# Layer 3's scans: two additions over states moved to GpSimd, one copy of exponents moved to VectorE

## The chip, the cores and the metric

The kernel runs on one core of a Trainium2 chip. A core has a matrix engine (TensorE, in the profile PE; its weight loads are PEld), three engines for elementwise work (VectorE = DVE, ScalarE = ACT, GpSimd = POOL) and SyncE (SP), which here only issues transfers. Each engine takes its instructions in the order of the program; engines wait for one another on semaphores. TensorE multiplies into PSUM, a small memory [...] that VectorE and ScalarE can read; everything else lies in SBUF (on chip) or DRAM. The metric is the time of one execution in microseconds (us), the median of three runs.

## The reference

The network has four layers on an input of 4 x 96 x 56 x 56 in float32. Layer 0 is attention, layer 1 a selective scan in eight directions, layer 2 a local attention. Layer 3, in which the change lies, contains a scan in four directions (rows, rows backwards, columns, columns backwards) over L = 56 x 56 = 3136 positions for 192 channels d and 16 states n, written with cumulative sums:

```
dlt = softplus(dt_proj(...) + dt_proj_b)
dA  = dlt[..., None] * A_log[None, :, :, None, :]
phi = jnp.exp(-jnp.cumsum(dA, axis=3))
dbx = dlt[..., None] * b[...] * xs[..., None]
h   = phi * jnp.cumsum(dbx / (phi + 1e-12), axis=3)
y   = jnp.einsum('bkdln,bknl->bkdl', h, c) + Ds
```

The sum over the 16 states n in the last line is the part that line 1446 to 1450 of the kernel compute; the exponents cumsum(dA) are what line 1375 copies.

## The kernel before

`network` (line 1662) runs the layers one after the other; `layer3` (line 1516) calls `cumulative` (line 1168), the stage that the change touches. It handles two directions at a time (k = 0, 1, then 2, 3). Positions are cut into chunks of 93 (`TW`), a chunk into three blocks of 31 positions (`TB`) plus one row of carry. A block holds 4 batch entries x 32 rows on the 128 partitions and 6 x 16 x 32 = 3072 values along the free axis. There are 2 x 34 = 68 chunk pairs, and so 68 x 3 x 2 = 408 blocks, the two directions in turn.

What happens to one block, with the names used below:

- `zhalf(st, h)`, line 1358, for h = 0 and 1: 48 matrix products of 32 x 32 x 256 (line 1367) give half of the block's exponents (8 of the 16 states) in the PSUM tile `z`, which has three banks and one buffer. Line 1375 copies the half, 128 x 1536 values, from PSUM to the block's `phi` in SBUF. "z0" and "z1" are the products of the two halves, "copy 0" and "copy 1" their copies. z1 can't start before copy 0 has emptied `z`.
- `inverse`, line 1383: ScalarE's sigmoid of `phi` into `w`. `phis`, line 1391: ScalarE's exponential of `phi` in place. The two need different tables (ACT_TABLE_LOAD).
- `weights`, lines 1399 to 1408: 16 small products into PSUM (`misc`), and on GpSimd a memset and two multiplications for `m`.
- `into_sum`, line 1415: VectorE multiplies `w` (SBUF) by `misc` (PSUM), 128 x 3072. Behind it SP's queue issues a transfer (line 1416) that puts the carry from DRAM (`l3cr`) into rows 31, 63, 95, 127 of `w`.
- `sums(st, q)`, line 1427, q = 0 to 3: 64 products give the cumulative sums of four states in PSUM (`q`, two buffers). They need `w` with its carry.
- `times(st, q)`, line 1436: VectorE multiplies them by `phi`, 128 x 768, result in `phi`.
- `carry`, line 1440: SP issues the transfer of the block's last row to `l3cr`.
- `out`, line 1442: three additions halve the 16 states to 2 (lines 1446, 1447 and 1448, into the tile `t`), a fourth (line 1450) makes `y`; SP issues four stores of `y` (line 1458).

The order on every engine is the order in which the program is written (`in_order`, line 53, ties each instruction to the one before it on its engine). The loop at line 1481 runs over pairs of blocks (`now`), with the next pair (`nxt`) and the one after (`third`) in work. One iteration handles block S of `now`, C = the block after S, and T = a block of `third`. VectorE's order in one iteration is: `times` S 0 and 1, `into_sum` C, `times` S 2 and 3, (scans of the next chunk), `out` S. TensorE's: `misc` of C, `sums` S 2 and 3, z0 of T, (products of the next chunk), z1 of T, `sums` C 0 and 1. ScalarE's: `inverse` or `phis` of one block, copy 0 of T, `inverse` or `phis` of the second block, copy 1 of T. GpSimd's: `m` of C, (work of the next chunk), `out` S. SP's: the carry into `w` of C (line 1416), the carry of S (line 1440), (loads of the next chunk), the stores of `y` (line 1458).

The next chunk is prepared in twelve steps (`tick`, lines 1503 and 1511), two an iteration, so that the six iterations of a chunk differ. In order of time: loads of `u`; two iterations with products of line 1229; one with the products of line 1256 and three softplus (line 1261 to 1263), the iteration in which `tick` says "wide" since these products use `z`'s banks, and z1 of T is put behind `sums` C; then two with a scan over time for one direction each: GpSimd's `du` (line 1298), VectorE's addition (line 1303, two inputs in SBUF), its scan (line 1311, two inputs in SBUF) and a small copy (line 1313), placed behind z1 and ahead of `out`. I call the six: loads, products 1, products 2, wide, scan 1, scan 2.

Of the kernel before, what the change touches and what calls it, by code (L numbers as in the profile page):

```python
# [11 lines left out]
ALU = mybir.AluOpType  # L12
# [19 lines left out]
def view(ap, offset, dims):  # L32

    return bass.AP(ap.tensor, ap.offset + offset, [ap.ap[0], *dims])
# [35 lines left out]
class Net:  # L70
# [1097 lines left out]
    def cumulative(self, us, dram):  # L1168


        nc, tc = self.nc, self.tc
# [6 lines left out]
        with in_order(tc), ExitStack() as cx:  # L1178
# [179 lines left out]
            def zhalf(st, h):  # L1358
                s, i = st["s"], st["i"]
                lo = TW - TB * (i + 1) if s["rev"] else TB * i  # L1360
                st["lo"] = lo
                z = psz.tile([128, 3, 2, 8, 32], F32, name="z")
                for dh in range(2):
                    for b in range(B):
                        for p in range(3):
                            ps_ = slice(32 * p, 32 * p + 32)
                            nc.tensor.matmul(  # L1367
                                z[32 * b : 32 * b + 32, p, dh].rearrange("p n d -> p (n d)"),
                                s["s"][ps_, dh, b, lo : lo + 32],
                                st["ad"][ps_, dh, 8 * h : 8 * h + 8, :].rearrange("p n d -> p (n d)"),  # L1370
                                start=True, stop=True,
                            )
                if h == 0:
                    st["phi"] = big.tile([128, 3, 2, NS, 32], F32, name="phi", bufs=5)
                nc.scalar.copy(  # L1375
                    st["phi"][:, :, :, 8 * h : 8 * h + 8, :].rearrange("p a b n d -> p a b (n d)"),
                    z.rearrange("p a b n d -> p a b (n d)"),
                )
# [63 lines left out]
            def out(st):  # L1442
                s, i, lo, k = st["s"], st["i"], st["lo"], st["k"]
                phi = st["phi"].rearrange("p a b n d -> p (a b) (n d)")
                t = p2.tile([128, 6, 8 * 32], F32, name="t", bufs=1)
                nc.vector.tensor_tensor(t, phi[:, :, 0:256], phi[:, :, 256:512], ALU.add)
                nc.vector.tensor_tensor(t[:, :, 0:128], t[:, :, 0:128], t[:, :, 128:256], ALU.add)  # L1447
                nc.gpsimd.tensor_tensor(t[:, :, 0:64], t[:, :, 0:64], t[:, :, 64:128], ALU.add)  # L1448
                y = p2.tile([128, DI], F32, name="y")
                nc.gpsimd.tensor_tensor(  # L1450
                    view(y, 0, [[32, 3], [96, 2], [1, 32]]),
                    view(t, 0, [[512, 3], [256, 2], [1, 32]]), view(t, 32, [[512, 3], [256, 2], [1, 32]]),
                    ALU.add,
                )
                a, e = max(lo, s["off"]), min(lo + TB, s["off"] + s["tv"])
                at = s["t0"] + a - s["off"]
                for b in range(B):
                    nc.sync.dma_start(
                        ys[k][b, at : at + e - a, :], y[32 * b + a - lo : 32 * b + e - lo, :]
                    )  # L1460
# [9 lines left out]
            for st in (*now, *nxt):  # L1470
                zhalf(st, 0)
                zhalf(st, 1)
# [8 lines left out]
            while now[0] is not None:  # L1481
                third = draw()
                for i, st in enumerate(now):
                    coming_up = (now[1], nxt[0])[i]
                    what = (inverse, phis)[i]
                    if nxt[0] is not None:
                        what(nxt[0])
                    if coming_up is not None:
                        weights(coming_up)
                    times(st, 0)  # L1490
                    times(st, 1)
                    sums(st, 2)
                    sums(st, 3)
                    if third[i] is not None:
                        zhalf(third[i], 0)
                    if nxt[1] is not None:
                        what(nxt[1])
                    if coming_up is not None:
                        into_sum(coming_up)
                    times(st, 2)  # L1500
                    times(st, 3)
                    carry(st)
                    wide = tick()[1]
                    if third[i] is not None and not wide:
                        zhalf(third[i], 1)
                    if coming_up is not None:
                        sums(coming_up, 0)
                        sums(coming_up, 1)
                    if third[i] is not None and wide:
                        zhalf(third[i], 1)  # L1510
                    tick()
                    out(st)
# [288 lines left out]
```

## Time and profile before

| | |
|---|---|
| time, median of 3 runs | 16318.02 us (16299.98 to 16343.79) |
| the profiled execution's own time | 16344.06 us |
| its span, first to last instruction | 16342.0 us |
| mean granted TensorE clock | 0.916 of full |
| the stage of the change, first to last row of line 1415 | 10712.4 to 15499.7 us |
| in the stretch 10700 to 15500 (4800 us) busy: PE, DVE, ACT, POOL | 4172, 4153, 4240, 1788 us |
| mean granted clock in that stretch | 0.93 |
| rows of line 1446 and 1447 (VectorE), mean | 408 x 1755 ns, 408 x 958 ns |
| rows of line 1448 and 1450 (GpSimd), mean | 408 x 998 ns, 408 x 590 ns |
| rows of line 1375 (ScalarE), mean | 816 x 1427 ns |
| rows of line 1436 and 1415 (VectorE), mean | 1632 x 953 ns, 408 x 3346 ns |
| rows of line 1311 (VectorE) and 1298 (GpSimd), median, mean | 136 x 1720 ns, 136 x 1807 ns |

A row of the timeline gives the start, the duration, the engine, the line, the operation, the tiles (out<-in), the shape and, in brackets, how long the engine stood idle before it and whose end released it. Rows of the same line close together are merged (x2). The view by windows gives, for each stretch of time, its length and the busy time of every engine in it, and then the granted clock (PEclk, 1.00 is full).

### The profile page before, as it was taken

The page shows a single profiled execution, that of the slowest core. Times are in us where ns is not written, and L with a number is a line of the kernel's source. Part 1 is how long each engine was busy: PE and PEld are TensorE (multiplying, and loading weights), DVE is VectorE, ACT ScalarE, POOL GpSimd, SP SyncE. Part 2 cuts the span into 40 slices and gives each one's busy share as a digit, 9 for nine tenths or more (in the row PEclk, how much of TensorE's full clock was granted, in tenths as well). Part 3 has the DMA queues.
Part 4 walks back from the last instruction along what each step waited for, and adds up shares of the span by engine and source line. Part 5 has one row for each costly group of instructions (what it writes and reads, how often), then busy time and mean ns, then how long its engine had stood idle before and what let it go on. Part 6 is the DMA issues. An engine that isn't in the chain of part 4 may idle for free.

```text
span 16342.0 us, 501766 instructions
## 1 busy us (share of the span) xinstructions
PE 13255.0 (81%) x222032; PEld 8983.5 (55%) x222032; DVE 13647.4 (84%) x15363; ACT 12214.4 (75%) x15540; POOL 7905.1 (48%) x4079
## 2 busy tenths in 40 slices
PE   8999977777777777777776678878888888888876
PEld 4333326666666666666665555446666656566543
DVE  8666549999999999999998666768888888888866
ACT  0465448999999999999998245478888888888822
POOL 0000028888888888888887022123333333333300
PEclk7999889999999999999999579989999999999977
DMA  0000034333444443434444910222122222222122
GB/s 15 1 1 1 16 137 100 92 92 92 102 105 105 104 93 93 95 92 103 104 106 105 220 41 10 63 61 50 48 51 50 50 50 49 50 50 51 41 67 65
DMA packets 821406, 1152.54 MB, mean 71 GB/s; under 512 B 309360, under 2 KB 728720, under 8 KB 807456
## 3 DMA queue, kind: packets, MB, share of 16 engines
q1 hardware_dynamic: 759872, 1055.38, 26.6%
q10 hardware_dynamic: 53984, 45.77, 1.2%
q8 instruction: 1746, 28.61, 0.8%
q0 software_dynamic: 5376, 19.27, 0.4%
q14 instruction: 428, 3.51, 0.1%
HBM read 842.93 MB, written 277.18 MB: 69 GB/s over the span
## 4 chain that ended last, share of the span: by engine, by line
PE 34%; DVE 29%; ACT 20%; issue 12%; DMA 4%; POOL 1%; SPq 1%; DVEq 0%; ACTq 0%; POOLq 0%
DVE q L634 17%; PE q L1427 7%; ACT ht L659 5%; PE s L233 4%; ACT e L622 3%; PE d L413 3%; ACT phi L1375 3%; DVE w L1415 3%; PE z L1367 2%; PE acc L251 2%; PE m L196 2%; ACT w L1383 2%; PE y L671 2%; PE t L557 2%; PE t L650 2%
## 5 line engine op out<-in xcount | busy, mean ns | idle before, releaser
L614 POOL TENSOR_TENSOR q<-du,bm 128x1792 f32<-128x1792 f32 x1344 | 5348.3, 4026 | 3.1 <-DMA bm<-bc 3.1
L634 DVE TENSOR_TENSOR_SCAN q<-e,state,q 128x448 f32<-128x448 f32 x4608 | 4876.8, 1124 | 145.9 <-ACT e L622 141.9
L622 ACT ACTIVATE e<-dl,na 128x448 f32<-128x448 f32 x5376 | 3354.9, 640 | 173.7 <-DVE q L634 117.8
L671 PE MATMUL y<-ht,cd 128*32 128x64 f32 x75264 | 1838.4, 225 | 1470.2 <-ACT ht L659 1469.6
L650 PE MATMUL t<-ident,q 128*128 128x128 f32 x18816 | 2626.8, 293 | 93.7 <-issue 77.6
L1427 PE MATMUL q<-w,m 32*32 32x192 f32 x52224 | 2573.4, 348 | 125.8 <-DVE phi L1436 72.9
L650 PEld LDWEIGHTS t<-ident,q 128*128 128x128 f32 x18816 | 2391.2, 203 | 325.3 <-issue 203.3
L659 ACT COPY ht<-t 128x896 f32<-128x896 f32 x2688 | 2428.6, 904 | 101.2 <-PE t L650 70.6
L671 PEld LDWEIGHTS y<-ht,cd 128*32 128x32 f32 x75264 | 1400.3, 110 | 1948.2 <-ACT ht L659 1930.7
L1427 PEld LDWEIGHTS q<-w,m 32*32 32x32 f32 x52224 | 1873.5, 113 | 738.1 <-issue 182.2
L1436 DVE TENSOR_TENSOR phi<-q,phi 128x768 f32<-128x768 f32 x1632 | 1513.5, 953 | 523.9 <-PE q L1427 498.3
L1448 POOL TENSOR_TENSOR t<-t 128x384 f32<-128x384 f32 x408 | 407.2, 998 | 2977.2 <-DVE t L1447 2977.2
L241 ACT ACTIVATE e<-s 128x896 f32<-128x896 f32 (+1 forms) x1050 | 921.8, 915 | 913.7 <-PE m L196 516.2
L1367 PE MATMUL z<-ad,sm 32*32 32x256 f32 x39168 | 1277.1, 391 | 396.2 <-ACT phi L1375 382.6
L208 DVE TENSOR_REDUCE pm<-m 128x1 f32<-128x448 f32 (+1 forms) x1700 | 997.8, 618 | 688.6 <-PE m L196 641.4
L1375 ACT COPY phi<-z 128x1536 f32<-128x1536 f32 x816 | 1164.5, 1427 | 528.6 <-PE z L1367 528.4
L1415 DVE TENSOR_TENSOR w<-w,misc 128x3072 f32<-128x3072 f32 x408 | 1365.3, 3346 | 83.9 <-PE misc L1399 46.9
L1383 ACT ACTIVATE w<-phi,lntiny,w_k_rmask 128x3072 f32<-128x3072 f32 x408 | 1203.1, 2949 | 2.6
L196 PE MATMUL m<-ka,qa 32*128 32x448 f32 (+1 forms) x3400 | 1165.9, 628 | 9.0 <-DVE pm L208 7.5
L1391 ACT ACTIVATE phi<-phi,w_k_nmask 128x3072 f32<-128x3072 f32 x408 | 1165.6, 2857 | 2.4
L1367 PEld LDWEIGHTS z<-ad,sm 32*32 32x32 f32 x39168 | 709.1, 104 | 658.9 <-ACT phi L1375 465.2
L292 POOL DMA_DIRECT2D x<-xc x28 | 14.5, 517 | 2153.7 <-DVE xc L291 2152.8
(254 smaller groups left out, 18732.7 us busy)
## 6 DMA issues: line engine op xcount, KB each, us to landing
bm<-bc SPq DMA_DIRECT2D x896, 448.0 KB
cm<-cd SPq DMA_DIRECT2D x544, 186.0 KB
l1y<-out SPq DMA_DIRECT2D x672, 96.0 KB
l1y<-out SPq DMA_DIRECT2D x672, 72.0 KB
y<-l1y ACTq DMA_DIRECT2D x224, 168.0 KB
l3y<-y SPq DMA_DIRECT2D x1616, 23.2 KB
w<-l3cr SPq DMA_DIRECT2D x408, 48.0 KB
l3cr<-phi SPq DMA_DIRECT2D x408, 48.0 KB
```

What stands on the lines that cost most here:

```text
L614: nc.gpsimd.tensor_tensor(q, spread(s["du"][:, j, :], ng), s["bm"][g], ALU.mult)
L622: nc.scalar.activation(e[:, :CH], s["dl"][:, j, :], AF.Exp, scale=na[:, s["k"], j, n : n + 1])
L634: nc.vector.tensor_tensor_scan(a, e, a, first, ALU.mult, ALU.add)
L650: nc.tensor.transpose(flat(t)[:, 128 * c : 128 * c + 128], view(q, h * NC2 + c, [[NC, 128]]), self.ident,)
L659: nc.scalar.copy(t, flat(s["t", j, g, h])[:, : NC2 * 128])
L671: nc.tensor.matmul(s["y", j][r : r + 32, c // 4, 64 * half : 64 * half + 64], s["cd"][:, half, g, c, :], s["t", j, g, h][:, 128 * i + 64 * ...
L1367: nc.tensor.matmul(z[32 * b : 32 * b + 32, p, dh].rearrange("p n d -> p (n d)"), s["s"][ps_, dh, b, lo : lo + 32], st["ad"][ps_, dh, 8 * h ...
L1375: nc.scalar.copy(st["phi"][:, :, :, 8 * h : 8 * h + 8, :].rearrange("p a b n d -> p a b (n d)"), z.rearrange("p a b n d -> p a b (n d)"),)
L1383: nc.scalar.activation(w.rearrange("p a n d -> p (a n d)"), st["phi"].rearrange("p a b n d -> p (a b n d)"), AF.Sigmoid, bias=lntiny, scal ...
L1415: nc.vector.tensor_tensor(st["w"], st["w"], ut, ALU.mult)
L1427: nc.tensor.matmul(qp[bs, n, :DI], st["m"][bs, 4 * q + n, :], st["w"][bs, :, 4 * q + n, :], start=True, stop=True,)
L1436: nc.vector.tensor_tensor(ph, view(st[q], 0, [[256, 4], [32, 6], [1, 32]]), ph, ALU.mult)
```

## The change

Three calls change their engine; no shape, tile, buffer count or place in the program changes.

```diff
@@ zhalf
                 if h == 0:
                     st["phi"] = big.tile([128, 3, 2, NS, 32], F32, name="phi", bufs=5)
-                nc.scalar.copy(
+                (nc.scalar.copy if h == 0 else nc.vector.tensor_copy)(
                     st["phi"][:, :, :, 8 * h : 8 * h + 8, :].rearrange("p a b n d -> p a b (n d)"),
                     z.rearrange("p a b n d -> p a b (n d)"),
                 )
@@ out
                 t = p2.tile([128, 6, 8 * 32], F32, name="t", bufs=1)
-                nc.vector.tensor_tensor(t, phi[:, :, 0:256], phi[:, :, 256:512], ALU.add)
-                nc.vector.tensor_tensor(t[:, :, 0:128], t[:, :, 0:128], t[:, :, 128:256], ALU.add)
+                nc.gpsimd.tensor_tensor(t, phi[:, :, 0:256], phi[:, :, 256:512], ALU.add)
+                nc.gpsimd.tensor_tensor(t[:, :, 0:128], t[:, :, 0:128], t[:, :, 128:256], ALU.add)
                 nc.gpsimd.tensor_tensor(t[:, :, 0:64], t[:, :, 0:64], t[:, :, 64:128], ALU.add)
```

Copy 1 goes from ScalarE to VectorE, where its place is behind `times` S 2 and 3 and ahead of the scan of the next chunk. The first two additions of `out` go from VectorE to GpSimd, where all four now stand in a row. The transfers that depend on them (the stores of `y` on SP's queue) keep their place in that queue.

## The prediction

> **What bounds the kernel now.** I read the page first: no engine is full over the span (PE 81%, DVE 84%, ACT 75%), so the stage has to be read by itself. Its length is 408 blocks; the starts of line 1415's rows give each iteration's length. Averaged over the inner 66 or so chunks, in us: loads 11.31, products 1 10.07, products 2 10.11, wide 15.13, scan 1 12.42, scan 2 11.42; sum 70.5 a chunk. The view by windows of one chunk (scan 1, scan 2, loads, products 1, products 2, wide) shows why they differ:
>
> ```profile
> core 0: us, PE busy (x) PEld busy (x) DVE busy (x) ACT busy (x) POOL busy (x), PEclk, DMA share, GB/s
> 12001.84:12014.90 13.06, 10.71 (x303) 8.76 (x302) 11.50 (x10) 13.00 (x9) 3.05 (x5) 0.87 0.07 20
> 12014.90:12026.31 11.41, 8.78 (x252) 6.25 (x248) 11.31 (x11) 10.04 (x6) 3.99 (x4) 1.00 0.07 19
> 12026.31:12038.29 11.98, 10.02 (x244) 7.17 (x240) 9.63 (x9) 10.52 (x6) 6.20 (x11) 0.86 0.28 68
> 12038.29:12048.47 10.18, 10.16 (x268) 6.88 (x264) 9.54 (x9) 7.78 (x7) 1.74 (x4) 1.00 0.09 24
> 12048.47:12058.59 10.12, 10.12 (x268) 6.86 (x264) 9.62 (x8) 10.09 (x8) 4.10 (x6) 1.00 0.09 25
> 12058.59:12072.59 14.00, 12.29 (x244) 7.64 (x240) 9.71 (x8) 11.14 (x9) 7.31 (x8) 0.88 0.52 123
> ```
>
> Only scan 2 is full on VectorE (11.31 of 11.41). Products 1 and 2 are a chain: `into_sum` C 3.34, carry into `w` by DMA 3.2, `sums` C 0 and 1 2.75, the last `times` 0.9: 10.2. Wide, and often scan 1 and loads, contain half-speed TensorE. So VectorE's time is worth money in two of six iterations at most. Next I read the timeline of scan 2, from `into_sum` C on:
>
> ```profile
> 12014.90 3.34 DVE L1415 TENSOR_TENSOR w<-w,misc 128x3072 f32<-128x3072 f32 x1
> ...
> 12018.16 1.82 DVE L1436 TENSOR_TENSOR phi<-q,phi 128x768 f32<-128x768 f32 x2
> ...
> 12018.37 1.44 ACT L1375 COPY phi<-z 128x1536 f32<-128x1536 f32 x1 [1.34 <-PE z L1367]
> ...
> 12019.86 1.36 PE L1367 MATMUL z<-ad,sm 32*32 32x256 f32 x48 [1.53 <-ACT phi L1375]
> 12019.89 0.16 DVE L1303 TENSOR_TENSOR dl<-dl,tot 96x8 f32<-96x8 f32 x1
> ...
> 12020.09 1.72 DVE L1311 TENSOR_TENSOR_SCAN sm<-starts,dl 96x752 f32<-96x752 f32 x1
> ...
> 12021.93 1.75 DVE L1446 TENSOR_TENSOR t<-phi 128x1536 f32<-128x1536 f32 x1
> ```
>
> To see here: VectorE ends `times` S 3 at 12019.9 (5.0 after the start of `into_sum`), but z1 ends only at 12021.22 (6.3), since it waited for copy 0. Last, the only place where VectorE works on two SBUF inputs while GpSimd works, near the stage's start:
>
> ```profile
> 10751.25 1.73 DVE L1303 TENSOR_TENSOR dl<-dl,tot 96x8 f32<-96x8 f32 x1 [9.14 <-POOL du L1298]
> 10753.01 2.68 DVE L1311 TENSOR_TENSOR_SCAN sm<-starts,dl 96x752 f32<-96x752 f32 x1
> 10755.72 0.83 DVE L1313 COPY tot<-sm 96x8 f32<-96x8 f32 x1
> ```
>
> The same three take 0.16, 1.72 and 0.17 elsewhere. Each ends when a GpSimd instruction (`du`, then line 1407, then line 1408, itself 2.35 in place of 1.05) has ended: they exclude each other, and GpSimd gets in between each two of the three. At 10671 the small copy takes 1.55 behind `du` twice.
>
> **Part 1, the additions.** VectorE loses 1.755 + 0.958 = 2.71 a block. GpSimd's price, from its rows 128x192 0.590, 128x384 0.998, 128x1344 3.055, 128x1792 4.02 (2.15 ns a value): 128x1536 3.47, 128x768 1.82. So `out` takes 3.47 + 1.82 + 1.0 + 0.59 + gaps = 7.2 from the end of `times` S 3, and `y` is ready at 5.05 + 7.2 = 12.3 in place of 9.5. GpSimd's load is 4.5 + 5.3, about 9.9 a block: under every iteration's length, if barely. Behind `y` in SP's queue stand four issues (1.4, to 13.7) and then the next carry into `w`, wanted at 10.1 + 3.4 = 13.5: 0.2 late, once in products, +0.3 a chunk. `phi` is read until 8.6, and its buffer is written next at 13.6: free of cost.
>
> **Part 2, copy 1.** ScalarE loses 1.43 a block (of 10.55). VectorE gains a copy from PSUM: the nearest rows are its copies of line 684 (128x384 0.544) and 260 (128x448 0.617); by the slope between those two (73 ns for 64 values) 128x1536 gives 1.86, by that of line 1446 and 1447 (1.04 ns a value) 1.75. I take 1.75, since rows with PSUM inputs (line 1436, 0.953) and without (line 1447, 0.958) cost the same there; the upper end adds 0.1. So VectorE's own sum falls by only 0.95. But the copy must wait for z1, and it stands ahead of the next scan and of `times` C.
>
> - Products, loads: z1 ends at 6.3 to 6.5, copy to 8.1 to 8.3, `sums` C 0 ends at 8.0, `sums` C 1 at 9.3. `times` C 1 starts at 9.3 as before: nothing gained, nothing lost.
> - Scans, without exclusion: 6.4 + 1.75 + 2.04 (scan) + 1.73 = 11.9 against 11.41: the wait of 1.4 exceeds the 0.95.
> - Wide: z1 ends 0.6 before the next `into_sum` today, as `times` C are long done. Now z1 is followed by copy 1.75 + 0.1 and two `times` 1.8, less the 0.6 and less 0.2 (copy 0 is earlier with a lighter ScalarE): +2.9, to 18.0.
>
> **Part 3, exclusion.** In scan 1 and 2 GpSimd is now in `out` (5.05 to 12.3) when VectorE wants line 1303, 1311 and 1313. The page SBUF — State Buffer of the Trainium skill, section "Who interferes with whom", speaks against the change here: a VectorE instruction with two SBUF inputs and a GpSimd instruction that reads SBUF block each other for a whole instruction, while one with a single SBUF input doesn't collide. The rows above are that, with short GpSimd instructions; so by them: copy 1 ends at 8.2, line 1303 waits for the first addition to 8.6; second addition to 10.5; scan to 12.25; third addition to 13.25; line 1313 to 13.4; `times` to 15.15. Were only the rest of the running addition lost, it would be 12.4; were there none, 11.9. I take 15.15, because in four cases of four in the trace GpSimd slipped in. Copy 1, `into_sum` and `times` have one input in PSUM; line 684's copy, under GpSimd's line 614 all the time, keeps 0.56.
>
> **The clock.** TensorE now idles 2.2 ahead of scan 1 (two `times` and a copy behind z1) and some 4 ahead of scan 2 and loads. The page TensorE: Matmul & The Clock Gate, section "Why this matters for your kernels", says that idle gaps up to about 3 us do no harm. The trace differs: in wide the gap between z0 and line 1256's products is 1.7 to 2.0, and every wide iteration measured has half clock. By the rule scan 1 stays at 15.15; by the row, half of them (as 61% of scan 1 today) lose 0.7, since slow `sums` push z0, z1 and copy 1: 15.5. Scan 2, idle 4, is 15.85 by both; loads go from 11.31 to 12.0 (its value with half clock today).
>
> **Sum.** Per chunk: wide +2.9, scan 1 +3.1, scan 2 +4.4, loads +0.7, products +0.3: +11.4. Times 67 (the last chunk prepares none): +760. Against the profiled execution's own 16344 that is 17104; against the median of 16318, 26 lower, **17078**; I say 17075.
>
> **The rivals.**
> - *No slipping in* (GpSimd doesn't get in between, or `out` is past when the scan comes): scans 12.4 and 12.3, so wide +2.9, scan 1 0, scan 2 +0.9, loads +0.3, products +0.3: +4.4, 16610. For it: only four cases, at the stage's start. Against: each of them.
> - *SP's queue*: if GpSimd's strided additions cost 2 us more than by the straight line (the row 128x384 is at 2.6 ns a value), the carry is 2.2 late in every short iteration and each second one pays: +3 more a chunk, and +2 in each scan: 17550 at most. Against: the rows of strided inputs lie within 0.03 of the line.
> - *Not slower: copy 1 is hidden.* If copy 0 came so early that z1 ended with `times` S 3, VectorE's 0.95 would be won in the scans (10.5), half clock would be gone from loads (10.27) and scan 1, and wide would keep 15.1: 66.6 a chunk, -3.9, 16060. It decides at z1 ending before 5.0 + 0.95 = 5.95, with no exclusion. The trace says 6.3, and z0 alone is 3.4 behind `into_sum`'s start. With the clock alone at full in wide (15.6 with the copy) and no exclusion it would be level with today, 16300.
>
> **How the numbers follow.** Exclusion as worked out, with more or less of the clock: 0.64, 16850 to 17300. No slipping in: 0.2. SP's queue: 0.1. Not slower: 0.06, of which 0.03 faster. The range reaches from within the second case, 16650, to 17350. A measurement can tell some 0.3% (49 us) from no change: slower 0.94, same 0.03, faster 0.03.
>
> **What would show it.** Right: line 1446 on GpSimd at 3.5, 1447 at 1.8; line 1303 and 1311 on VectorE far above 0.16 and 1.72 in most of the 136; scan iterations near 15; wide near 18; copy 1 on VectorE idle 1.3 before it by PE z; products still 10.1. Wrong: line 1303 and 1311 unchanged (then 16610); SP waiting for `y` with line 1416 issued late in products; a clock above 0.93 in the stage.

## The result, and the profile after

The changed kernel takes 17045.03 us (median of 4 runs, 17032.57 to 17049.84) where the kernel before takes 16315.32 (median of 4, 16299.98 to 16343.79): ratio 1.044, 95% interval 1.0427 to 1.0453. The profiled execution took 17032.57 with a span of 17030.8 and a mean granted clock of 0.909. The stage, first to last row of line 1415, went from 4787.3 us to 5537.2 (10647.8 to 16185.0): +749.9 us. The rest of the profiled span was 61 us shorter: the layers ahead of the stage, which the change doesn't touch, ended earlier. In the traces of this case the stage begins anywhere from 10638 to 10712, a spread that no term of the forecast contained.

Iteration lengths, mean over the inner chunks in us; in brackets, how much of the iteration had a granted clock near half:

| | loads | products 1 | products 2 | wide | scan 1 | scan 2 | chunk |
|---|---|---|---|---|---|---|---|
| before | 11.31 [2.1] | 10.07 | 10.11 | 15.13 [5.5] | 12.42 [2.1] | 11.42 [0.1] | 70.47 |
| after | 11.42 [2.8] | 11.40 | 11.27 | 18.64 [7.2] | 13.88 [2.0] | 15.06 [5.7] | 81.66 |
| measured change | +0.1 | +1.3 | +1.2 | +3.5 | +1.5 | +3.6 | +11.2 |
| predicted | +0.7 | +0.3 for both | | +2.9 | +3.1 | +4.4 | +11.4 |

11.2 times 67 chunks is 750, the whole of the stage's growth. The sum is as predicted; its terms are not.

The view by windows of one chunk, this time in the order products 2, wide, scan 1, scan 2, loads, products 1:

```profile
core 0: us, PE busy (x) PEld busy (x) DVE busy (x) ACT busy (x) POOL busy (x), PEclk, DMA share, GB/s
13005.36:13017.10 11.74, 10.25 (x267) 6.87 (x263) 8.66 (x7) 9.74 (x7) 9.77 (x9) 1.00 0.08 22
13017.10:13035.58 18.48, 14.51 (x256) 8.35 (x252) 8.48 (x7) 12.03 (x9) 13.53 (x12) 0.82 0.41 100
13035.58:13049.27 13.69, 9.26 (x292) 6.89 (x285) 12.37 (x10) 8.74 (x5) 8.30 (x4) 0.92 0.04 10
13049.27:13065.03 15.76, 12.53 (x256) 8.36 (x252) 11.57 (x10) 8.42 (x4) 13.74 (x12) 0.75 0.06 16
13065.03:13076.40 11.37, 9.80 (x244) 6.50 (x240) 8.67 (x8) 8.03 (x4) 6.70 (x6) 0.85 0.28 69
13076.40:13087.61 11.21, 10.25 (x268) 6.86 (x263) 8.66 (x7) 8.07 (x7) 8.91 (x8) 1.00 0.09 22
```

VectorE is now lighter (8.66 in products) and full nowhere (12.37 of 13.69 at most, time that it was blocked included); GpSimd has risen to 7 to 14. No engine's load explains 18.48 or 15.76: what grew are waits between engines. Products are longer at a clock of 1.00, so there it isn't the clock.

The timeline of scan 1, VectorE and GpSimd from the end of `times` S 3 on:

```profile
13040.74 3.46 POOL L1446 TENSOR_TENSOR t<-phi 128x1536 f32<-128x1536 f32 x1 [7.35 <-DVE phi L1436]
...
13041.91 1.76 DVE L1375 COPY phi<-z 128x1536 f32<-128x1536 f32 x1 [1.25 <-issue]
...
13043.58 0.64 DVE L1303 TENSOR_TENSOR dl<-dl,tot 96x8 f32<-96x8 f32 x1
...
13044.26 1.72 DVE L1311 TENSOR_TENSOR_SCAN sm<-starts,dl 96x752 f32<-96x752 f32 x1
13044.27 3.32 POOL L1447 TENSOR_TENSOR t<-t 128x768 f32<-128x768 f32 x1
...
13046.01 1.61 DVE L1313 COPY tot<-sm 96x8 f32<-96x8 f32 x1
```

VectorE and GpSimd exclude each other here, as forecast: line 1303 ends when line 1446 ends (13044.2), line 1447 (1.82 by itself) takes 3.32 since it waits for the scan, and line 1313 (0.17 by itself) waits for line 1447. But between line 1303 and line 1311 GpSimd did not get in: the scan kept its 1.72. Copy 1 itself runs under line 1446 undisturbed, 1.76.

The timeline of wide, from copy 1 on, after and then before:

```profile
13032.18 1.76 DVE L1375 COPY phi<-z 128x1536 f32<-128x1536 f32 x1 [10.00 <-POOL m L1408]
13033.85 1.81 DVE L1436 TENSOR_TENSOR phi<-q,phi 128x768 f32<-128x768 f32 x2
...
13034.95 2.59 PE L1427 MATMUL q<-w,m 32*32 32x192 f32 x57 [2.39 <-DVE phi L1436]
```

```profile
12070.96 0.96 DVE L1436 TENSOR_TENSOR phi<-q,phi 128x768 f32<-128x768 f32 x1 [1.31 <-PE q L1427]
...
12072.09 1.44 ACT L1375 COPY phi<-z 128x1536 f32<-128x1536 f32 x1 [2.82 <-PE z L1367]
...
12072.59 3.35 DVE L1415 TENSOR_TENSOR w<-w,misc 128x3072 f32<-128x3072 f32 x1 [0.67 <-PE misc L1399]
```

VectorE stood idle for 10.00 us ahead of copy 1. The bracket names line 1408, which had ended 0.5 earlier and whose output the copy doesn't read; what the copy waited for is z1, whose products ended at 13032.1. Behind the copy stand two `times` whose input had been ready since 13030.8, and TensorE's next sums wait for those (2.39). Before, the two `times` were done ahead of z1's end (12072.05), and the next `into_sum` did not wait for the copy. After, it begins at 13035.6. From z1's end to the next `into_sum` it is 0.54 before and 3.50 after, in the mean of all wide iterations.

Last, products 2: SP's queue and the first product that needs the carry, after and then before.

```profile
13006.73 1.39 SPq L1458 DMA_DIRECT2D l3y<-y  x4
...
13008.73 0.50 SPq L1416 DMA_DIRECT2D w<-l3cr  x1
...
13013.37 2.80 PE L1427 MATMUL q<-w,m 32*32 32x192 f32 x64 [1.49 <-DMA w<-l3cr]
```

```profile
12048.34 1.41 SPq L1458 DMA_DIRECT2D l3y<-y  x4
...
12051.83 0.50 SPq L1416 DMA_DIRECT2D w<-l3cr  x1
...
12054.86 2.80 PE L1427 MATMUL q<-w,m 32*32 32x192 f32 x64
```

After, the carry is issued 2.0 behind the start of the stores (13006.73) and used 4.64 after its issue; before, 3.5 behind and used 3.03 after its issue. It isn't issued late in either: `into_sum` ends at 13008.70. It lands late. The DMA records show the stores' 124 packets of 768 bytes running until 3.62 after the carry's issue (before: 2.02). The carry itself is four packets of 12288 bytes. Three of them end 2.0 to 2.14 after the issue in both kernels; the fourth begins when the stores' last packet has ended, and ends at 4.09 (before: 2.48). TensorE uses the carry 0.55 behind that end in both. It is so throughout: in products 2 the stores' last packet ends 3.46 after the carry's issue and the carry's fourth at 3.93 (medians; before, 1.83 and 2.29).

### The profile page after: what moved, and what is told of

It reads as the page before. It is cut to its first block, busy times and chain, and to the rows that moved or that the text cites. A ratio compares the mean times of both kernels' runs of the same rounds, so it can differ in the third digit from the quotient of the medians.

```text
span 17030.8 us, 501969 instructions
## 1 busy us (share of the span) xinstructions
PE 13449.8 (79%) x222032; PEld 9029.1 (53%) x222032; DVE 13446.7 (79%) x14955; ACT 11692.7 (69%) x15132; POOL 10242.9 (60%) x4895
## 5 line engine op out<-in xcount | busy, mean ns | idle before, releaser
L1427 PE MATMUL q<-w,m 32*32 32x192 f32 x52224 | 2725.5, 362 | 715.0 <-DVE phi L1436 525.8
L1427 PEld LDWEIGHTS q<-w,m 32*32 32x32 f32 x52224 | 1935.4, 118 | 1459.7 <-issue 485.0
L1446 POOL TENSOR_TENSOR t<-phi 128x1536 f32<-128x1536 f32 x408 | 1406.1, 3446 | 1323.6 <-DVE phi L1436 1317.2
L1375 ACT COPY phi<-z 128x1536 f32<-128x1536 f32 x408 | 586.9, 1438 | 1814.3 <-issue 1206.8
L1375 DVE COPY phi<-z 128x1536 f32<-128x1536 f32 x408 | 717.1, 1758 | 1312.1 <-POOL m L1408 561.5
```

Of the source, the lines that this page charges most:

```text
L1375: (nc.scalar.copy if h == 0 else nc.vector.tensor_copy)(st["phi"][:, :, :, 8 * h : 8 * h + 8, :].rearrange("p a b n d -> p a b (n d)"), z. ...
L1427: nc.tensor.matmul(qp[bs, n, :DI], st["m"][bs, 4 * q + n, :], st["w"][bs, :, 4 * q + n, :], start=True, stop=True,)
L1446: nc.gpsimd.tensor_tensor(t, phi[:, :, 0:256], phi[:, :, 256:512], ALU.add)
```

## The experiments

The theory was that of the prediction: copy 1 holds up VectorE in wide, the additions block the scans' VectorE instructions. The rival, formed from the table above: a good part is due to neither, but to `y` coming later, so that its stores stand directly ahead of the carry. Times below are medians; ratios stand against the kernel before.

**Additions alone: copy 1 back on ScalarE.**

```diff
-                (nc.scalar.copy if h == 0 else nc.vector.tensor_copy)(
+                nc.scalar.copy(
```

> Only the additions move to GpSimd; copy 1 is ScalarE's again. Theory (three separate costs: copy 1's wait in VectorE's queue, the exclusion of GpSimd and VectorE, and the stores of y just ahead of the carry in the DMA queue): wide falls back to 15.1 us, products stay at 11.3 since y is as late as in the changed kernel, scan 1 and 2 stay above before (12.3 to 14.0) with lines 1311 and 1313 far above 1.72 and 0.17: 16600 to 16800 us. Rival 1 (GpSimd with its 10 us a block is simply the bound): as the changed kernel, 17045. Rival 2 (copy 1 is the whole cost, the additions are free or a gain): 16315 or less.

Measured: 16823.51, ratio 1.030 [1.0278, 1.0323], 24 us above the range expected. Chunk 77.73: loads 11.77, products 11.76 and 11.67, wide 15.60, scans 13.45 and 13.49. So the additions alone cost 7.3 a chunk, of which 3.25 in the two products. The timeline of its scan 1:

```profile
13022.58 0.16 DVE L1303 TENSOR_TENSOR dl<-dl,tot 96x8 f32<-96x8 f32 x1
13022.75 3.45 POOL L1446 TENSOR_TENSOR t<-phi 128x1536 f32<-128x1536 f32 x1 [2.72 <-DVE dl L1303]
13022.78 5.00 DVE L1311 TENSOR_TENSOR_SCAN sm<-starts,dl 96x752 f32<-96x752 f32 x1
13026.27 3.11 POOL L1447 TENSOR_TENSOR t<-t 128x768 f32<-128x768 f32 x1
13027.81 1.60 DVE L1313 COPY tot<-sm 96x8 f32<-96x8 f32 x1
```

Here line 1446 was ready 0.03 ahead of the scan, and the scan waited for all of it: 5.00. In the changed kernel line 1447 came 0.01 behind the scan and waited instead. Over the 134 scans of the stage in each of the two kernels: where a GpSimd row begins 0.006 or more ahead of line 1311 and still runs, line 1311 has a median of 5.00 (132 of this kernel's) and 2.52 (32 of the changed kernel's, 29 of them behind line 1448); where none does, 1.72 (the other 102 of the changed kernel's). So the one that begins first goes first, by these rows.

**Copy 1 alone: both additions back on VectorE.**

```diff
-                nc.gpsimd.tensor_tensor(t, phi[:, :, 0:256], phi[:, :, 256:512], ALU.add)
-                nc.gpsimd.tensor_tensor(t[:, :, 0:128], t[:, :, 0:128], t[:, :, 128:256], ALU.add)
+                nc.vector.tensor_tensor(t, phi[:, :, 0:256], phi[:, :, 256:512], ALU.add)
+                nc.vector.tensor_tensor(t[:, :, 0:128], t[:, :, 0:128], t[:, :, 128:256], ALU.add)
```

> Only copy 1 moves to VectorE; the additions are VectorE's again. Theory: copy 1 waits for z1 and the additions then stand behind it, so every iteration is 2.7 us or so longer than in the changed kernel without its other costs: products 12.8, scans 14.6, loads 12.8, wide 21: about 17500 us, no exclusion in the rows of lines 1303, 1311, 1313. Rival 2 (copy 1 is the whole cost and the additions are free wherever they are): 17045. Rival 1 (GpSimd is the bound): about 16315.

Measured: 17979.31, ratio 1.1013 [1.0988, 1.1038]; chunk 95.54, all six iterations longer (13.78, 12.64, 14.03, 21.63, 16.50, 16.97). With the additions on VectorE, they stand behind copy 1, and the copy waits for z1: in loads, for example, a copy at 13032.69, line 1446 at 13034.36, line 1447 at 13036.15, and only at 13037.02 the `times` that TensorE waits for. It is slower than expected; every scan and 65 of 66 products 2 now contain half clock too, which I hadn't counted. The two halves of the change aren't additive: 25.1 and 7.3 a chunk alone, 11.2 together.

**Stores late: the changed kernel with the stores of `y` issued behind the next carry.**

```diff
@@ out
-                y = p2.tile([128, DI], F32, name="y")
+                y = p2.tile([128, DI], F32, name="y", bufs=3)
...
-                for b in range(B):
-                    nc.sync.dma_start(
-                        ys[k][b, at : at + e - a, :], y[32 * b + a - lo : 32 * b + e - lo, :]
-                    )
+                held.append((ys[k], y, a, e, at, lo))
@@ the main loop, directly behind carry(st)
+                    stores()
```

`stores()` issues what is held. So SP's order is carry into `w`, carry of S, stores. The third buffer of `y` is there since the stores are held; in the changed kernel no row of line 1450 waits for a buffer (each starts 0.08 behind line 1448).

> The changed kernel with the four stores of y issued behind the next iteration's two carries (y with three buffers), nothing else moved. Theory (the stores' packets stand ahead of the carry's in the DMA queue, so it lands 1 us or more later): products fall from 11.3 to 10.1, the wait of line 1427 for the carry falls from 146 us to some 30, the rest is unchanged: 16315 + 730 - 165 = 16880 us. Rival 1 (products are long because GpSimd is the bound): 17045.

Measured: 16952.86, ratio 1.0383 [1.0365, 1.0402]. Products are 10.07 and 10.07, as before the change (10.07 and 10.11). In the iteration of products 2 at 13005.3 the carry is used 3.04 after its issue; over all of them the four packets end by 2.13 (median). The wait of line 1427 for the carry, between 10640 and 16190 us of each trace, falls from 171.0 us (168 times) to

```profile
PE q L1427 <- DMA w<-l3cr: 21.7, 15, 7.6
```

(us, times, the longest). That is the rival's share shown: 2.5 a chunk, caused by what is queued ahead of the carry. The time fell by less than expected, as 1.1 came back on balance: loads 12.03, scan 1 14.41 and scan 2 15.42 each contain more half clock than in the changed kernel (4.3, 3.6 and 7.4 us an iteration).

**Two additions left out.** Lines 1446 and 1447 are left out and line 1448 adds straight from `phi`, so the sum over states is incomplete; copy 1 stays on VectorE.

```diff
-                nc.gpsimd.tensor_tensor(t, phi[:, :, 0:256], phi[:, :, 256:512], ALU.add)
-                nc.gpsimd.tensor_tensor(t[:, :, 0:128], t[:, :, 0:128], t[:, :, 128:256], ALU.add)
-                nc.gpsimd.tensor_tensor(t[:, :, 0:64], t[:, :, 0:64], t[:, :, 64:128], ALU.add)
+                nc.gpsimd.tensor_tensor(t[:, :, 0:64], phi[:, :, 0:64], phi[:, :, 64:128], ALU.add)
```

> The changed kernel without the first two additions (lines 1446 and 1447 are left out, the third takes its inputs from phi; the sums over states are then incomplete). Theory (exclusion and late y are the additions' costs): scans 12.0 to 12.5 with lines 1303, 1311, 1313 at 0.16, 1.72, 0.17 or near, products 10.1, wide 18.5 as in the changed kernel: 16500 to 16600 us. Rival (the scans are long through copy 1's wait for z1 alone): scans stay at 13.7 to 15, only products fall: 16880.

Measured: 16547.01, ratio 1.0129 [1.0106, 1.0151]. Chunk 73.89: wide 18.26 (+3.1), scan 1 12.44 (0), scan 2 12.31 (+0.9), products 10.08 and 10.05, loads 10.76. Lines 1303, 1311 and 1313 take 0.16, 1.72 and 0.17. This is the price of copy 1 with nothing beside it. The terms are those of the prediction's rival of no slipping in (2.9, 0, 0.9), though in the scans not for its reason, as no addition runs here: scan 2 took 11.69 in the 16 of 66 iterations at full clock and 12.51 in the others.

**Memsets in place of the two additions.** GpSimd is as busy as with them (5.7 us in place of 5.3), but reads nothing from SBUF meanwhile. The one-column copy makes the memsets wait for `phi`, as the additions did. The sum over states is incomplete here too.

```diff
-                nc.gpsimd.tensor_tensor(t, phi[:, :, 0:256], phi[:, :, 256:512], ALU.add)
-                nc.gpsimd.tensor_tensor(t[:, :, 0:128], t[:, :, 0:128], t[:, :, 128:256], ALU.add)
-                nc.gpsimd.tensor_tensor(t[:, :, 0:64], t[:, :, 0:64], t[:, :, 64:128], ALU.add)
+                nc.gpsimd.tensor_copy(t[:, 5, 0:1], phi[:, 5, 511:512])
+                for _ in range(4):
+                    nc.gpsimd.memset(t, 0.0)
+                nc.gpsimd.tensor_tensor(t[:, :, 0:64], phi[:, :, 0:64], phi[:, :, 64:128], ALU.add)
```

> The changed kernel with the two additions replaced by a one-column copy from phi and four memsets of t on GpSimd, of about the same total time, which write SBUF but read nothing (the sums over states are incomplete). Theory (exclusion comes from GpSimd's reads against VectorE's second SBUF input): lines 1303 and 1311 back at 0.16 and 1.72, line 1313, a copy with one input, perhaps still waiting; scans 12 to 13.5; products still 11.3, since y is as late: 16700 to 16800 us. Rival (any GpSimd instruction excludes): the rows stay long and the time stays at 17045.

Measured: 17079.05, ratio 1.0457 [1.0434, 1.0481]. The timeline of its scan 1:

```profile
13066.40 5.69 POOL L1448 MEMSET t<- 128x1536 f32 x4
...
13069.01 0.16 DVE L1303 TENSOR_TENSOR dl<-dl,tot 96x8 f32<-96x8 f32 x1
...
13069.21 1.72 DVE L1311 TENSOR_TENSOR_SCAN sm<-starts,dl 96x752 f32<-96x752 f32 x1
...
13070.96 1.15 DVE L1313 COPY tot<-sm 96x8 f32<-96x8 f32 x1
```

The rows are as the theory has it: under four memsets lines 1303 and 1311 keep 0.16 and 1.72, so neither GpSimd's being busy nor its writing blocks them; what the additions do besides is read. The small copy of line 1313 still takes 0.78 to 1.15 in nearly all scans, which the theory as I had put it doesn't explain (the last section returns to it). The time is not as expected: scan 1 fell to 13.06, but in products `y` comes 0.6 later than with the additions, and products (11.80, 12.01), wide (19.37) and loads (12.03) each rose. The run shows the exclusion in the rows; as a measure of its price in the total it failed.

**Only the second addition moved**, from the kernel before: copy 1 on ScalarE, line 1446 on VectorE, line 1447 on GpSimd.

```diff
-                nc.vector.tensor_tensor(t[:, :, 0:128], t[:, :, 0:128], t[:, :, 128:256], ALU.add)
+                nc.gpsimd.tensor_tensor(t[:, :, 0:128], t[:, :, 0:128], t[:, :, 128:256], ALU.add)
```

> The kernel before with one edit: only the second addition (line 1447) on GpSimd; line 1446 and copy 1 stay where they were. Theory: in the scan iterations VectorE is the bound and its trio (lines 1303, 1311, 1313) is over before GpSimd starts, so nothing excludes anything; VectorE loses 0.96 and scan 2 falls from 11.42 to 10.5, scan 1 by 0.4 to 1.0; y comes 0.9 later, which products hardly feel: 16315 minus 90 to 130, some 16210 us. Rival (any addition moved to GpSimd costs through y's lateness or GpSimd's slower rate): 16315 or more.

Measured: 16551.21, ratio 1.0141 [1.0118, 1.0164]. The theory fell here. Scan 2 did get faster (10.68 in place of 11.42), but loads rose from 11.31 to 14.58. The timeline of loads:

```profile
13065.03 1.39 SPq L1458 DMA_DIRECT2D l3y<-y  x4
13066.59 0.48 SPq L1416 DMA_DIRECT2D w<-l3cr  x1
...
13072.02 5.34 PE L1427 MATMUL q<-w,m 32*32 32x192 f32 x64 [2.90 <-DMA w<-l3cr]
```

With a shorter scan 2 its stores come right ahead of the carry of loads, 1.56 before it; the carry's fourth packet ends 4.55 and the carry is used 5.43 after its issue, and then the 64 products take 5.34 in place of 2.80: half clock, from 13071.0 on, behind gaps of 1.5 and 2.90 on TensorE.

**The same with the stores late** (edits of the two runs together), and, as a control, **the stores late in the kernel before**.

> The run with only the second addition on GpSimd, with the stores of y issued behind the next iteration's two carries. Theory (that run lost its 1.4% in the loads iteration alone, 14.58 us in place of 11.31, since scan 2's stores stood right ahead of the carry, the carry landed some 2 us late and TensorE's clock then halved): loads back to 10.3 to 11.4, products 2 from 10.63 to 10.1, scan 2 still 10.4 to 10.7: 16270 to 16350 us, the kernel before or a trifle less. Rival (loads is long because scan 2 is short, whatever the stores do: TensorE or ScalarE hold it): 16550.

> The kernel before with the stores of y behind the next carries and nothing else: a control. Theory: in the kernel before y's packets are gone when the carry is issued, so nothing is to be won: within 0.3% of 16320. Rival (late stores help or hurt by themselves, as they moved loads and the scans up by 0.5 us in the changed kernel): 1 us a chunk either way, 70 us.

Measured: 16174.0, ratio 0.9911 [0.9895, 0.9927], and 16314.71, ratio 0.9992 [0.9981, 1.0003]. The late stores alone gain nothing; with the second addition on GpSimd they turn 1.4% slower into 0.9% faster, more than expected. The timeline of loads, in place of the last one:

```profile
13081.29 0.48 SPq L1416 DMA_DIRECT2D w<-l3cr  x1
...
13083.57 1.67 SPq L1465 DMA_DIRECT2D l3y<-y  x4
13084.04 2.80 PE L1427 MATMUL q<-w,m 32*32 32x192 f32 x64
```

Loads take 10.13 with 0.3 of half clock, scan 2 10.46; chunk 68.44, 2.03 less than before, times 67 is 136 of the measured 142. Line 1311 has 1.73 on average, line 1313 0.17: line 1447 begins only behind VectorE's line 1446, so it never meets the scan.

**Copy 1 back on ScalarE in wide alone**, all else as changed.

```diff
-            def zhalf(st, h):
+            def zhalf(st, h, wide=False):
...
-                (nc.scalar.copy if h == 0 else nc.vector.tensor_copy)(
+                (nc.scalar.copy if h == 0 or wide else nc.vector.tensor_copy)(
...
-                        zhalf(third[i], 1)
+                        zhalf(third[i], 1, True)
```

> The changed kernel with copy 1 of the wide iteration alone back on ScalarE. Theory (in wide the copy stands behind the softplus and ahead of two times, a new wait of some 3.3 us once a chunk): wide 18.6 to 15.2, the rest unchanged: 17045 - 67 x 3.3 = 16825 us. Rival (wide is long because TensorE's clock is half there, whoever copies): 17045.

Measured: 16843.3, ratio 1.0318 [1.0294, 1.0343]. Wide falls from 18.64 to 15.60, with as much half clock as in the changed kernel (7.0 us, 7.2 there), and from z1's end to the next `into_sum` it is 0.54 again: the copy in wide costs 3.0, and it is all of wide's growth but 0.5. The chunk falls by as much, from 81.66 to 78.71; the other iterations move by up to 1.2 either way and offset.

**Each edit only where it can pay** (edits against the changed kernel): copy 1 on VectorE in loads and products, line 1446 on GpSimd there, line 1447 on GpSimd everywhere; first with the stores late in loads and products alone, then everywhere.

```diff
+                early = 2 * st["i"] + st["k"] % 2 < 3
-                (nc.scalar.copy if h == 0 else nc.vector.tensor_copy)(
+                (nc.vector.tensor_copy if h == 1 and early else nc.scalar.copy)(
...
+                both = 2 * st["i"] + st["k"] % 2 in (2, 3, 4)
-                nc.gpsimd.tensor_tensor(t, phi[:, :, 0:256], phi[:, :, 256:512], ALU.add)
+                (nc.gpsimd if both else nc.vector).tensor_tensor(t, phi[:, :, 0:256], phi[:, :, 256:512], ALU.add)
```

> Each move only where the iteration has room: in loads and both products copy 1 on VectorE, both additions on GpSimd and the stores of y behind the next carries; in wide and the scans copy 1 on ScalarE, line 1446 on VectorE, only line 1447 on GpSimd. Theory: products 10.1, scan 2 10.5, scan 1 11 (ScalarE no longer late after products), wide 14.5: -1 to -3 us a chunk, 16110 to 16250 us. Rival (ScalarE's relief is worth nothing since the clock sets wide and scan 1): as the run with only the second addition moved.

> The run by iteration with all stores behind the next carries, those of the scans and wide too. Theory: loads falls from 13.04 to about 11, the rest stays: 73.0 - 2 = 71 a chunk, 16300 to 16370 us. Rival (half clock in wide and scan 1 takes it back): 16460.

Measured: 16464.66, ratio 1.008 [1.0058, 1.0101], and 16140.73, ratio 0.9895 [0.9877, 0.9914], the fastest of all. The first is 200 us slower than expected, as the stores of scan 2 still stood ahead of the carry of loads; the second is 160 us faster. Between the two lies only the place of the stores in wide and the scans: loads 13.10 to 10.09, wide 15.48 to 14.47, scan 2 11.39 to 10.44. Of the six, only wide is shorter than in the kernel with the second addition and late stores (15.09) by more than 0.05, and scan 1 is 0.25 longer; the two kernels' intervals overlap, so the other edits show no gain over the second addition with late stores.

## Why the prediction was right, and where its terms were not

- **Wide, +2.9 predicted, +3.5 measured.** The mechanism is shown by the copy put back in wide alone (3.0 of it) and by the run with two additions left out (3.1). The other 0.5 is there with the additions alone too (15.60), where copy 1 isn't moved: it comes with the additions.
- **Products, +0.3 predicted, +2.5 measured.** This is the term that failed. The step was: the carry is issued 0.2 late behind four stores. `y` was ready at 12.3, as worked out, but the issue was not late; the transfer took 4.64 to its use in place of 3.03, as one of the carry's four packets began only behind the stores' last. I had taken the carry's 3.2 from a trace in which the stores were issued 3.5 ahead of it, and kept it where my own sum put them 1.4 ahead. The late stores get all 2.5 back, which shows the cause. By the Trainium skill (DMA: Bandwidth & Descriptors, "Queues, rings and completion order") a completion lands only after every earlier write of the same DMA engine; the records agree with that, but they show more: the carry's fourth packet itself began at 3.62, so it is the packet that was late and not its completion alone.
- **Scan 1, +3.1 predicted, +1.5 measured.** The step was that GpSimd gets in between each two of lines 1303, 1311 and 1313. It got in once. In the iteration shown copy 1, line 1303, the scan and line 1313 ended 8.1, 8.6, 10.4 and 12.0 after the start, and the iteration was over at 13.7; I had 8.2, 8.6, 12.25, 13.4 and 15.15. I had made a rule of the cases at the stage's start, and called them the only ones. They weren't: at 10669.49 in the trace before, a scan began 0.03 ahead of `du` and kept its 1.72, and `du` waited. The page that I cited for the exclusion (SBUF — State Buffer, "Who interferes with whom") says, in a point I passed over, that whichever instruction is issued first blocks the other; the rows above agree, and in 102 of 134 scans no GpSimd row began more than 0.005 ahead of line 1311.
- **Scan 2, +4.4 predicted, +3.6 measured**, nearer than its parts. The changed kernel's own iterations tell them apart. In the 17 of 66 at full clock scan 2 took 13.66, with 4.01 in its three lines in place of 2.05: that is the 11.69 of the run without additions at full clock, and 1.96 of exclusion. In the other 49 it took 15.54, with 3.02 in the three lines. So exclusion cost 1.0 there, and 2.9 go with half clock. In the mean of all 66 that is 0.3 for copy 1, 1.2 for exclusion, where I had 3.25, and 2.1 for the clock, to which I had given 0.7. With half clock z0 is slow and copy 1 begins later (9.2 after the start in the 49, 6.3 in the 17), so that more of the additions are past when the scan comes. This split is worked out from iterations of one trace; no run changed the clock alone.
- **Loads, +0.7 predicted, +0.1 measured.** Half clock is in 77% of them (61% before), 2.8 us in place of 2.1, at little cost.
- **The clock.** The rule of the Trainium skill (TensorE: Matmul & The Clock Gate, "Why this matters for your kernels") would have left loads alone in the run that moved the second addition only, with gaps of 1.5 and 2.9; their sums took 5.34 in place of 2.80. The row of wide was the better guide: in the stage before, 150 of 152 stretches of half clock have no gap above 3 us on TensorE in the 7 us ahead of them. No run changed the clock by itself, so how much half clock follows a gap of a given length stays open, and with it what exactly the late stores gave back.

Products and wide, 2.8 too low together, offset the scans and loads, 3.0 too high: that the total came within 0.2% is luck. Two of the signs that the prediction named for being right did not come: products went to 11.3 in place of 10.1, and the scan itself was far above 1.72 in 32 of 134 cases, not in most. What is right in it is wide, and that VectorE and GpSimd exclude each other at a cost in both scans. (ScalarE's load is 10.4 a block by the profile, 4240 over 408, and not 10.55; nothing rests on it.) The late-`y` mechanism that the products term left out is also what decides the smaller changes tried here.

## What to carry to other kernels

Work that is moved off a full engine makes its result later, and what counts is what is queued behind that result: here four small stores just ahead of a carry that TensorE waits for. Issue a transfer that someone waits for ahead of bulk stores; by itself that gained nothing (0.9992), but it decided the sign of the addition worth moving (1.0141 against 0.9911). And place an instruction that waits for another engine behind those whose input is ready: one copy of 1.76 us, ahead of two `times` that were ready, cost 3.0 us in each wide iteration. Moving the copy behind them was not tried; putting it back on ScalarE was.

## What was new about the hardware

- A transfer's time depends on what was issued on the same queue just before it. One of the carry's four packets began only when the last of the stores' 124 had ended, whose run takes 4.9 us. With the stores issued 3.5, 2.0 and 1.56 ahead, the carry's last packet ended 2.48, 4.09 and 4.55 us after its issue, and TensorE used it at 3.03, 4.64 and 5.43; with the stores behind it, all four packets ended by 2.13.
- A lead of some hundredths of a microsecond decides which of VectorE and GpSimd blocks the other: the same scan took 1.72 where the addition came 0.01 behind it and 5.00 where it came 0.03 ahead.
- The copy of 96 x 8 values, with a single input in SBUF, waits too: 0.17 alone, 1.61 behind an addition, 0.78 to 1.15 under memsets, which leave the scan at 1.72. In the prediction I had let every single input pass. The same SBUF section excepts copies within SBUF, which can take both ports; these rows agree, and so does copy 1, with its input in PSUM, at 1.76 under line 1446.
